# Two quarters of a weight transform moved into the groups that use them, in a gated scan and Hadamard feed-forward kernel

## The chip, the cores and the metric

The kernel runs on one core of one Trainium2 chip, with its engines TensorE (PE; PEld is its weight load), VectorE (DVE), ScalarE (ACT), GpSimd (POOL) and SyncE (SP, which here only issues DMAs). The metric is device microseconds of one execution. Everything is float32.

## What is computed

Four sequences of 512 tokens with 512 channels pass a gated linear scan and then a feed-forward block with 2048 hidden channels, each with a normalized residual. Cut to what matters:

```python
x = x + layernorm(attn(layernorm(x)))
x = x + layernorm(ffn(layernorm(x)))

def attn(h):                       # h: (4, 512, 512)
    i, f, g = h @ Wi.T, h @ Wf.T, h @ Wg.T
    gate = sigmoid(f)
    v = silu(i) * (1 - gate)
    o = scan over tokens: o[t] = gate[t] * o[t-1] + v[t]
    return (rmsnorm(o) * gnorm_w * g * sigmoid(g)) @ Wo.T

def ffn(x):                        # W1, W3: (2048, 512); W2: (512, 2048)
    hidden = silu(x @ W1.T) * (x @ W3.T)
    hidden = walsh_hadamard(hidden)         # along 2048 channels, / sqrt(2048)
    return hidden @ W2.T
```

## The kernel before

Every large product is done by the seven-product scheme for 2x2 block matrices (Strassen in Winograd's form): `ORDER` names the products P1, P2, P6, P5, P7, P3, P4 with their left and right operands. Of the left operand's seven blocks A11, A12, A21, A22 are data and S1, S2, S4 sums (`combine_left`; S3 takes A21's place); of the right operand's, B11, B21, B22, B12 are data and T1, T2, T4 sums (`combine_right`; T3 takes B12's place). A product adds into one of three PSUM banks X, Y, Z; after each product a copy on ScalarE (the first into a target) or an addition on VectorE takes the bank to SBUF: line 524 or 522 in projections and output products, 960 or 963 in the paired groups.

The Hadamard transform is not applied to the hidden channels but to W2, on which it works as well. Its high part is done by matmuls in the first 100 us and written to the DRAM tensor `w2_h`. The low part is done per quarter p = 0..3 of 512 hidden channels: `load_low(p)` loads four pieces of 256 KB (line 1109) into two tiles, `low_pair(p)` adds and subtracts the two tiles (lines 1120 and 1121, four VectorE instructions), and `low_tile(m)` makes the seven blocks of a tile's right operand in place (lines 1127 to 1134: five VectorE instructions and one on ScalarE), and writes them to DRAM (`kept`, line 179, issued by GpSimd, 896 KB). `again` (line 186) reads such a kept tile back.

The order of the work, by sequence (batch) b:

- `attn_unit(b, u)` for u = 0, 1, 2 projects with Wi, Wf, Wg; `attn_out(b)` multiplies by Wo. Work given to `fill` is put between the products of a unit; work in `beside` stands at a named product of it, behind an instruction that `behind(...)` names.
- Batches 0 and 1 do the first half of the hidden channels alone: `solo_unit(b, m)`, m = 0..3, with `ffn_out(b, 0)` and `ffn_out(b, 1)` for the first two quarters of W2. Batch 3's attention (units at about 226 to 290 us) lies between `solo_unit(0, 3)` and `solo_unit(1, 0)`.
- The rest is done for two sequences at once by `ffn_pair`, with one more level of the seven-product scheme over the pair. `GROUPS = 2, 3, 0, 1, 2, 3`: groups at = 0 and 1 are quarters 2 and 3 for the pair (0, 1), groups 2 to 5 all four quarters for the pair (2, 3). The first group starts at about 356 us, the second at 425, the third at 493.

A group has seven steps (`OUTER`: P1, P2, P6, P7, P5, P4, P3), each of seven products ("leaves", 1 to 49 in a group). A step's left operand is a "leaf weight" (tag "w" of the pool `stream`): four pieces of 128 KB are loaded per step from the kept W1 and W3 by `load_leaf_w`, three steps ahead, and summed on GpSimd. Its right operand is a token block: `xq[B11]`, `xq[B21]`, and so on, each of seven inner blocks. `blocks[0]` holds the pair B11 and B12, `blocks[1]` B21 and B22, `blocks[2]` T2 and T1; T4 has a tile of its own. Raw differences (`raw`, `combine_pair_early`, `combine_pair_late`) make T2, T1, T3, T4 out of the four data blocks, and `inner` makes the inner sums of a token block, in this kernel for the two blocks of a pair in one instruction. The dictionary `events` gives what is put behind a leaf. Between the leaves stand the output products of the group before (`down`, `ffn_out` in pieces). After steps 5 and 6, `hidden` multiplies the gates into the tiles `ht` (line 930), whose inner sums GpSimd makes.

The third quarter's low transform is loaded before `attn_unit(3, 0)` and done beside `attn_unit(3, 1)`; the last quarter's beside `solo_unit(1, 0)`. Both are kept in DRAM, and `load_down_pair(2)` and `load_down_pair(3)` read them back at leaf 14 of the groups 0 and 1.

W1 and W3 of the hidden channels' second half are prepared in eight calls of `prepare()` from `solo_unit(0, 3)` to `solo_unit(1, 3)`: load two of 256 KB into a tile of `stream` (lines 198), sum on VectorE (`combine_weights`, lines 158 to 163), write to DRAM (line 179).

Buffers: `stream` has five tiles (unit weights, prepared weights, leaf weights), `stream2` four (W2's quarters and Wo). The tag "wide" of the pool `work` has three: outputs of the two sequences (`f_0`, `f_1`) hold two of them through the pair's two groups; the third goes from an attention output `y` to the normalized rows of batch 3 (`xn_f_3`, written to DRAM at line 317) and, in the second group, to the first fold of the next pair (`load_half_fold(0)`). A "fold" is a reload of normalized rows from DRAM in the order in which VectorE transposes them (line 460 loads, 485 transposes).

TensorE's and SP's instructions run in the order in which the program gives them. Those of VectorE, ScalarE and GpSimd are put in order by a planner, with its own estimates of when each is ready, priorities (`tc.high_priority`) and "not before" edges (`tc.issue_after`); on the chip each engine then runs its list in order. A DMA issued on SP waits there until its tile is free, and everything behind it on SP waits too.

Of the kernel before, what the change touches and what calls it, by code (L numbers as in the profile page):

```python
# [11 lines left out]
F32 = mybir.dt.float32  # L12
# [32 lines left out]
def kernel(  # L45
# [119 lines left out]
    def combine_right(t, eng, steps=(0, 1)):  # L165

        if 0 in steps:
            eng.tensor_sub(t[:, T1], t[:, B12], t[:, B11])
            read["T2"] = eng.tensor_sub(t[:, T2], t[:, B22], t[:, T1])
        if 1 in steps:  # L170
            eng.tensor_sub(t[:, T3], t[:, B22], t[:, B12])
        if 0 in steps:
            eng.tensor_sub(t[:, T4], t[:, B21], t[:, T2])

    def kept(key, t):

# [4 lines left out]
    def stream_tile(key, b, pool=stream):  # L181
        return pool.tile([P, 7, H], F32, tag="w", name="_".join(map(str, (*key, b))))
# [3 lines left out]
        nc.sync.dma_start(out=t, in_=saved[key])  # L186
        return t

    def weight(src, name, m, b):

        key = name, m
        if key in saved:
            return again(key, b).rearrange("p s (c f) -> p s c f", c=2)
        t = stream_tile(key, b)
        half = src.shape[1] // 2
        for h in range(2):
            cols = slice(h * half + m * P, h * half + (m + 1) * P)
            nc.sync.dma_start(
                out=t[:, 2 * h : 2 * h + 2].rearrange("p k (c f) -> p (k c) f", c=2),
                in_=src[:, cols].rearrange("(p c) f -> p c f", p=P),  # L200
            )
        uncombined.append((key, t))
        return t.rearrange("p s (c f) -> p s c f", c=2)
# [600 lines left out]
    def raw(r):  # L804
        return xq[r][:, 0:4]

    def inner(pair, steps=(0, 1), eng=None):
        combine_right(pair.rearrange("p r s f -> p s r f"), eng or nc.vector, steps)

    def combine_pair_early():  # L810

# [286 lines left out]
    def load_low(p):  # L1098


        ms = range(p * NS, (p + 1) * NS)
        if p == 1:
            pair = work.tile([P, NS, 7, H], F32, tag="og", name="w2_23")
            tiles = [pair[:, k] for k in range(NS)]
        else:
            tiles = [stream_tile(("w2", m), 0, stream2) for m in ms]
        for n, k in ((1, 4), (0, 0)):
            for m, t in zip(ms, tiles):
                nc.sync.dma_start(
                    out=t[:, k : k + 2].rearrange("p k f -> p (k f)"),  # L1110
                    in_=w2_h[:, n * NU + m, :],
                )
        for m, t in zip(ms, tiles):
            down_w[0, m] = low_w[m] = t

    def low_pair(p):

# [188 lines left out]
    def prepare():  # L1306
        name, m = LATER.pop(0)
        weight(SOURCE[name], name, m, 0)
# [48 lines left out]
    attn_unit(3, 1)  # L1357
    combine_soon()
# [6 lines left out]

    places = (1, "P2"), (4, "P7"), (6, "P3")
    fill.extend([None] * 4 + attn_out(3))
    load_low(3)
    spread_low(3, "P2", 0)
    prepare()  # L1370
    solo_unit(1, 0, True)
    for b in PAIR:
# [13 lines left out]
        + [lambda: [make() for make in early]],  # L1386
        places,
    )
    prepare()
    solo_unit(1, 2)  # L1390
    fill.extend([None] + ffn_out(1, 0))
    pair_beside([partial(inner, blocks[0]), partial(inner, blocks[1], (0,))], places)
    prepare()
    for k in range(AHEAD):
        load_leaf_w(k)
    solo_unit(1, 3)
# [1 line left out]
        folds.pop(("f", b))  # L1398


    late = combine_pair_late()
# [14 lines left out]
    def exchange():  # L1416
# [3 lines left out]
    ffn_pair(  # L1420
        1,
        down,
        {
            7: [partial(load_half_fold, 0)],
            9: [partial(load_half_fold, 1)],
            14: [partial(load_down_pair, 3)],
            29: [transpose_half(0, 0, half_fold(0, 0))],
            31: [transpose_half(1, 0, half_fold(1, 0))],
            37: [exchange, transpose_half(0, 1, half_fold(0, 1))],
            39: [transpose_half(1, 1, half_fold(1, 1))],  # L1430
            43: [partial(early_step, 0)],
            45: [partial(early_step, 1)],
            47: [partial(early_step, 2)],
            49: [partial(early_step, 3)],
        },
        28,
    )
# [8 lines left out]
    PAIR[:] = 2, 3  # L1446
    for at in range(2, len(GROUPS)):
        g = GROUPS[at]
        ffn_pair(at, deque(down), {**late, 24: [partial(load_down_pair, g)]})
        late = {}  # L1450
        down = [part for b in PAIR for part in ffn_out(b, g, True)]
    for b in PAIR:
# [35 lines left out]
```

## Time and profile before

| what | value |
|---|---|
| time, median of 3 runs | 799.63 us (798.67 to 799.67) |
| profiled execution, its own time | 800.42 us |
| its span, first to last instruction | 798.6 us |
| mean granted TensorE clock | 0.991 |
| PE busy | 768.2 us (96%), 3552 matmuls |
| PEld busy | 662.4 us (83%) |
| DVE busy | 615.9 us (77%), 1157 instructions |
| ACT busy | 238.2 us (30%) |
| POOL busy | 350.5 us (44%) |
| DMA | 149.12 MB, 187 GB/s over the span |
| kept tile to DRAM (line 179, 896 KB) | 24 times, median 7.7 us from issue to landing |
| prepared or unit weight from the inputs (256 KB) | 32 times, 5.9 us |
| leaf weight piece (128 KB) | 168 times, 2.4 us |
| low transform piece (256 KB) | 16 times, 8.1 us |

Busy shares of the span in five stretches, worked out from the windows' sums (the last column is the mean granted clock):

| stretch, us | what runs | PE | DVE | POOL | clock |
|---|---|---|---|---|---|
| 200 to 264 | end of batch 0's solo units, batch 3's first attention units | 58.0 of 64.0 | 48.8 | 12.6 | 1.00 |
| 264 to 355.8 | rest of batch 3's attention, batch 1's solo units | 89.0 of 91.8 | 76.9 | 13.9 | 1.00 |
| 355.8 to 425.4 | first group of the first pair | 65.3 of 69.6 | 55.4 | 44.1 | 0.95 |
| 425.4 to 493.1 | second group | 67.3 of 67.7 | 54.2 | 47.9 | 1.00 |
| 493.1 to 560 | third group's first part | 64.8 of 66.9 | 55.9 | 51.3 | 1.00 |

A row of a view names the source line, the engine, the operation, and what is written from what (out<-in). A wait is written as who waited and for whom. An instruction's row in a timeline may merge several of one kind; its length then goes from the first to the last.

### The profile page before, as it was taken

What the parts mean: (1) busy time and instruction counts of PE and PEld (TensorE: products, weight loads), DVE (VectorE), ACT (ScalarE), POOL (GpSimd) and SP (SyncE); (2) the same over time, 40 slices, a digit from 0 to 9 for tenths busy, and PEclk for the clock granted to TensorE, in tenths of its full rate; (3) what the DMA queues carried; (4) which work ended last, traced back from release to release, by engine and by line L of the source; (5) the groups of instructions that cost most, each with busy time, mean ns of one, the idle gap of its engine ahead of it and who ended that gap; (6) DMA issues with size and microseconds to landing.
All of it is one profiled execution on the core that took longest, in us unless ns stands there. A gap on an engine that the chain in (4) does not pass through costs nothing.

```text
span 798.6 us, 10396 instructions
## 1 busy us (share of the span) xinstructions
PE 768.2 (96%) x3552; PEld 662.4 (83%) x3552; DVE 615.9 (77%) x1157; ACT 238.2 (30%) x332; POOL 350.5 (44%) x429
## 2 busy tenths in 40 slices
PE   9999999999998999897999999899999999999994
PEld 7888688887887788786888888788888788888884
DVE  6789889799686797899767599977755655765686
ACT  5373745535534332324111111021230201121112
POOL 2111203013202100048469558957966865682452
PEclk9999999999999999999999999999999999999998
DMA  9997556885998989868229320243455141124012
GB/s 302 398 340 294 168 195 224 264 277 198 372 323 302 347 319 325 327 225 303 74 66 253 87 57 27 74 136 94 106 171 132 53 143 55 54 70 154 1 53 105
DMA packets 93908, 149.12 MB, mean 187 GB/s; under 512 B 15136, under 2 KB 72096, under 8 KB 93600
## 3 DMA queue, kind: packets, MB, share of 16 engines
q1 hardware_dynamic: 82992, 97.87, 39.4%
q0 software_dynamic: 10144, 49.29, 17.0%
q10 hardware_dynamic: 720, 1.31, 0.4%
q8 instruction: 28, 0.46, 0.2%
q14 instruction: 24, 0.20, 0.1%
HBM read 100.21 MB, written 50.33 MB: 188 GB/s over the span
## 4 chain that ended last, share of the span: by engine, by line
PE 75%; DVE 11%; DMA 7%; POOL 2%; issue 2%; SPq 1%; ACT 1%; POOLq 0%; DVEq 0%
PE X_u L950 16%; PE X_po L715 10%; PE X_a L547 8%; PE Z_u L950 8%; PE Z_po L715 5%; PE X_f L547 5%; PE Z_a L547 4%; PE Y_u L950 4%; PE X_y L655 3%; PE Y_po L715 2%; PE Y_a L547 2%; PE Z_f L547 2%; DMA wl<-s_w 2%; DMA fold_a<-xnd_a 2%; PE Z_y L655 2%
## 5 line engine op out<-in xcount | busy, mean ns | idle before, releaser
L715 PE MATMUL X_po<-w,ht 128*128 128x256 f32 x512 | 140.8, 383 | 0.4 <-DVE f L522 0.3
L963 DVE TENSOR_TENSOR q<-X_u,q 128x512 f32<-128x512 f32 x132 | 90.7, 687 | 52.2 <-PE X_u L950 50.0
L950 PE MATMUL X_u<-xq,wl 128*128 128x256 f32 x480 | 123.6, 381 | 4.8 <-ACT q L960 2.8
L715 PEld LDWEIGHTS X_po<-w,ht 128*128 128x128 f32 x512 | 98.3, 192 | 14.8 <-DVE f L522 1.2
L950 PEld LDWEIGHTS X_u<-xq,wl 128*128 128x128 f32 x480 | 91.2, 191 | 18.7 <-DVE q L963 2.8
L921 ACT ACTIVATE q<-q 128x1024 f32<-128x1024 f32 x24 | 25.4, 1058 | 157.8 <-DVE q L963 89.0
L878 POOL TENSOR_TENSOR q<-q,q 128x512 f32<-128x512 f32 x48 | 60.6, 1277 | 26.2 <-DVE q L963 24.4
L715 PE MATMUL Z_po<-w,ht 128*128 128x256 f32 x256 | 69.1, 379 | 1.0 <-ACT f L524 1.0
L963 DVE TENSOR_TENSOR q<-Z_u,q 128x512 f32<-128x512 f32 x72 | 49.6, 689 | 25.5 <-PE Z_u L950 24.6
L179 POOL DMA_DIRECT2D s_w<-w x24 | 13.1, 547 | 118.6 <-DVE w L163 89.8
L547 PE MATMUL X_f<-xt_f,w 128*128 128x256 f32 x256 | 60.6, 381 | 4.1 <-DMA w<-s_w 2.7
L960 ACT COPY q<-X_u 128x512 f32<-128x512 f32 x36 | 21.0, 585 | 143.6 <-PE X_u L950 139.4
L950 PE MATMUL Z_u<-xq,wl 128*128 128x256 f32 x240 | 61.6, 379 | 0.0
L547 PEld LDWEIGHTS X_f<-xt_f,w 128*128 128x128 f32 x256 | 48.2, 190 | 11.8 <-DMA w<-s_w 3.1
L715 PEld LDWEIGHTS Z_po<-w,ht 128*128 128x128 f32 x256 | 48.5, 190 | 8.1 <-ACT f L524 1.4
L950 PE MATMUL X_u<-og,wl 128*128 128x256 f32 x192 | 50.1, 384 | 2.3 <-DVE q L963 2.2
L950 PEld LDWEIGHTS Z_u<-xq,wl 128*128 128x128 f32 x240 | 45.6, 190 | 6.2
L158 POOL TENSOR_TENSOR wl<-wl 128x256 f32<-128x256 f32 x42 | 33.6, 800 | 38.7 <-DMA wl<-s_w 32.1
L522 DVE TENSOR_TENSOR f<-X_po,f 128x512 f32<-128x512 f32 x51 | 34.9, 683 | 12.5 <-PE X_po L715 11.7
L950 PEld LDWEIGHTS X_u<-og,wl 128*128 128x128 f32 x192 | 36.7, 193 | 8.8 <-POOL wl L163 2.6
L963 DVE TENSOR_TENSOR q<-Y_u,q 128x512 f32<-128x512 f32 x42 | 28.8, 687 | 19.2 <-PE Y_u L950 17.8
L930 DVE TENSOR_TENSOR ht<-q 128x512 f32<-128x512 f32 x48 | 38.3, 820 | 5.3 <-PE X_po L715 4.1
(221 smaller groups left out, 1573.1 us busy)
## 6 DMA issues: line engine op xcount, KB each, us to landing
s_w<-w POOLq DMA_DIRECT2D x24, 896.0 KB, 7.7
w<-s_w SPq DMA_DIRECT2D x24, 896.0 KB, 7.3
wl<-s_w SPq DMA_DIRECT2D x168, 128.0 KB, 2.4
w<-in_W_dram SPq DMA_DIRECT2D x32, 256.0 KB, 5.9
wi<-s_wi SPq DMA_DIRECT2D x6, 896.0 KB, 8.8
wf<-s_wf SPq DMA_DIRECT2D x6, 896.0 KB, 8.1
wg<-s_wg SPq DMA_DIRECT2D x6, 896.0 KB, 7.1
w_h<-w2p POOLq DMA_DIRECT2D x8, 512.0 KB, 5.8
```

Source lines behind the costliest of these rows:

```text
L158: eng.tensor_add(t[:, S1], t[:, A21], t[:, A22])
L179: nc.gpsimd.dma_start(out=saved[key], in_=t)
L522: read[what] = nc.vector.tensor_add(to, ps[which], to)
L547: nc.tensor.matmul(ps[:, n, :], w[:, a, c, :], xt[:, bb, c, :], start=first and n == 0 and c == 0, stop=c == 1, skip_group_check=True,)
L655: nc.tensor.matmul(ps[:, t, :], og[:, a, c, ts(t, P)], w[c][:, bb, :], start=first and t == 0 and c == 0, stop=c == 1, skip_group_check=True,)
L715: nc.tensor.matmul(ps[:, t, :], hts[b, m][:, a, ts(t, P)], w[m][:, W2[bb], :], start=first and k == 0, stop=m == ms[-1], skip_group_check= ...
L878: queued.append(make(*args).ins)
L921: nc.scalar.activation(d[:, 0], d[:, 0], AF.Silu)
L930: nc.vector.tensor_mul(t[:, h : h + 3 : 2], d[:, 0, n].rearrange("p (t f) -> p t f", t=2), d[:, 1, n].rearrange("p (t f) -> p t f", t=2),)
L950: nc.tensor.matmul(ps[which][:, k, :], w[:, k, a, :], x[:, bb, :], start=first and k == 0, stop=True, skip_group_check=True,)
L960: read["copy"] = nc.scalar.copy(y, ps[which])
L963: last = nc.vector.tensor_add(y, ps[which], z)
```

## The change

1. *Low transform.* `load_low`, `low_pair` and `low_tile` of quarter 2 leave batch 3's attention units and become events of the first group (load at leaf 6, pair at 17, tiles at 19 and 23). Those of quarter 3 leave `solo_unit(1, 0)` and become events of the second group (leaves 1, 10, 12, 14). The tiles are used where they are made, for both sequences (`down_w[1, m]` too), and are still written to DRAM for the second pair. `load_down_pair` at leaf 14 of the two groups is gone.
2. *Inner sums.* `inner` takes one token block instead of a pair. B11's are made beside `solo_unit(1, 3)`; those of B21, T2, B12, T1, T4, B22 become events at leaves 2 to 35 of a pair's first group. For the second pair, B11's first three are made on GpSimd (behind leaf 36 of the second group) and the fourth on VectorE at leaf 45; the two calls behind the second group are gone.
3. *Prepared weights.* The last two (W1 and W3 of m = 7) are no longer prepared in `stream` beside `solo_unit(1, 2)` and `solo_unit(1, 3)`. `prepare_wide` loads them into tiles of the tag "wide": the first before the first group's first leaf, the second at leaf 14; their sums stand at leaves 13 and 25.
4. *Batch 3's attention input.* Its four normalizing copies stand at earlier products ((0, 3), (0, 4), (0, 6), (1, 0) in place of (0, 4), (0, 5), (1, 0), (1, 3), where the pair is unit and product), and `load_fold(3, "a", "x")` goes ahead of `load_attn_w(3, 0)`.

```diff
-    def weight(src, name, m, b):
+    def weight(src, name, m, b, t=None):
...
-        t = stream_tile(key, b)
+        if t is None:
+            t = stream_tile(key, b)
...
-    def inner(pair, steps=(0, 1), eng=None):
-        combine_right(pair.rearrange("p r s f -> p s r f"), eng or nc.vector, steps)
+    def inner(r, steps=(0, 1), eng=None):
+        return combine_right(xq[r], eng or nc.vector, steps)
...
             1: [partial(sub, raw(T2), raw(B21), raw(T4))],
-            2: [partial(sub, raw(T1), raw(B22), raw(T2))],
-            4: [partial(inner, blocks[1], (1,))],
-            6: [partial(inner, blocks[2], (0,))],
-            8: [partial(inner, blocks[2], (1,))],
-            11: [partial(combine_right, xq[T4], nc.vector)],
+            2: [partial(inner, B21, (0,))],
+            5: [partial(sub, raw(T1), raw(B22), raw(T2))],
+            7: [partial(inner, B21, (1,))],
+            9: [partial(inner, T2)],
+            15: [partial(inner, B12)],
+            21: [partial(inner, T1)],
+            28: [partial(inner, T4)],
+            35: [partial(inner, B22)],
...
-            down_w[0, m] = low_w[m] = t
+            down_w[0, m] = down_w[1, m] = low_w[m] = t
...
-    late = dict(beside_copies(3, ((0, 4), (0, 5), (1, 0), (1, 3))))
+    late = dict(beside_copies(3, ((0, 3), (0, 4), (0, 6), (1, 0))))
...
+    load_fold(3, "a", "x")
     load_attn_w(3, 0)
-    load_fold(3, "a", "x")
     load_low(1)
...
     load_attn_w(3, 1)
-    load_low(2)
...
-    spread_low(2, "P2", 0)
...
-    load_low(3)
-    spread_low(3, "P2", 0)
...
-    prepare()
     solo_unit(1, 2)
     fill.extend([None] + ffn_out(1, 0))
-    pair_beside([partial(inner, blocks[0]), partial(inner, blocks[1], (0,))], places)
-    prepare()
+    pair_beside([partial(inner, B11)], places)
...
+    def low_beside(p, leaves):
+        makes = [partial(load_low, p), partial(low_pair, p)]
+        makes += [partial(low_tile, NS * p + t) for t in range(NS)]
+        return {leaf: [make] for leaf, make in zip(leaves, makes)}
+
+    def prepare_wide():
+        name, m = LATER.pop(0)
+        t = work.tile([P, 8, H], F32, tag="wide", name=f"{name}_{m}", bufs=3)
+        weight(SOURCE[name], name, m, 0, t[:, 0:7])
+
     load_down_w(1, 1)
+    prepare_wide()
+    late = merged(
+        combine_pair_late(),
+        {13: [combine_weights], 14: [prepare_wide], 25: [combine_weights]},
+        low_beside(2, (6, 17, 19, 23)),
+    )
...
-    ffn_pair(0, deque(down), {**late, 14: [partial(load_down_pair, 2)]})
+    ffn_pair(0, deque(down), late)
...
-            14: [partial(load_down_pair, 3)],
...
+            36: [partial(in_order, inner, B11, (0,), nc.gpsimd)],
...
-            45: [partial(early_step, 1)],
+            45: [partial(inner, B11, (1,)), partial(early_step, 1)],
...
-        },
+        }, low_beside(3, (1, 10, 12, 14))),
         28,
     )
-    with tc.high_priority(offset=SOON):
-        inner(blocks[0])
-        inner(blocks[1], (0,))
```

`merged` joins several such dictionaries, leaf by leaf; `combine_right` now returns the instruction that it issues last.

More of the change, by code (lines that the diff above doesn't have):

```diff
@@ L172, in combine_right @@
         if 0 in steps:
-            eng.tensor_sub(t[:, T4], t[:, B21], t[:, T2])
+            return eng.tensor_sub(t[:, T4], t[:, B21], t[:, T2])
     def kept(key, t):
@@ L830, in combine_pair_late, with merged @@
             1: [partial(sub, raw(T2), raw(B21), raw(T4))],
-            2: [partial(sub, raw(T1), raw(B22), raw(T2))],
-            4: [partial(inner, blocks[1], (1,))],
-            6: [partial(inner, blocks[2], (0,))],
-            8: [partial(inner, blocks[2], (1,))],
-            11: [partial(combine_right, xq[T4], nc.vector)],
-        }
+            2: [partial(inner, B21, (0,))],
[6 more added lines that the diff above has]
+            35: [partial(inner, B22)],
+        }
+    def merged(*plans):
+        events = {}
+        for plan in plans:
+            for leaf, makes in plan.items():
+                events.setdefault(leaf, []).extend(makes)
+        return events
     def pair_beside(makes, places):
@@ L1398 @@
         folds.pop(("f", b))
-    late = combine_pair_late()
-    load_down_w(1, 1)
+    def low_beside(p, leaves):
[6 more added lines that the diff above has]
+        weight(SOURCE[name], name, m, 0, t[:, 0:7])
+    load_down_w(1, 1)
+    prepare_wide()
[4 more added lines that the diff above has]
+    )
     down = [make for make in fill if make] + ffn_out(1, 1, True)
     fill.clear()
-    ffn_pair(0, deque(down), {**late, 14: [partial(load_down_pair, 2)]})
+    ffn_pair(0, deque(down), late)
     down = deque(part for b in PAIR for part in ffn_out(b, 2, True))
@@ L1422 @@
         down,
-        {
+        merged({
             7: [partial(load_half_fold, 0)],
             9: [partial(load_half_fold, 1)],
-            14: [partial(load_down_pair, 3)],
             29: [transpose_half(0, 0, half_fold(0, 0))],
             31: [transpose_half(1, 0, half_fold(1, 0))],
+            36: [partial(in_order, inner, B11, (0,), nc.gpsimd)],
             37: [exchange, transpose_half(0, 1, half_fold(0, 1))],
@@ L1448 @@
         g = GROUPS[at]
-        ffn_pair(at, deque(down), {**late, 24: [partial(load_down_pair, g)]})
+        ffn_pair(at, deque(down), merged(late, {24: [partial(load_down_pair, g)]}))
         late = {}
```

## The prediction

> **What bounds the kernel now.** I read the page first: TensorE is busy 768.2 of 798.6 us, and its 3552 matmuls come every 0.216 us where nothing is late (8 in 1.73 us in the chain that ended last). 3552 x 0.216 = 767, so all there is to win is some 31 us in which TensorE stands or runs at a lower clock. Next I read what TensorE waited for. The columns are us in total, times, longest.
>
> ```profile
> PE X_u L950 <- DVE q L963: 4.2, 2, 2.2
> PE X_a L547 <- ACT d_a L524: 3.1, 1, 3.1
> PE X_u L950 <- ACT q L960: 2.8, 2, 2.1
> PE X_f L547 <- DMA w<-s_w: 2.7, 1, 2.7
> PE X_a L547 <- DVE d_a L522: 1.5, 1, 1.5
> PE X_a L547 <- issue: 1.4, 1, 1.4
> PE X_f L547 <- DVE d_f L522: 1.4, 1, 1.4
> ```
>
> The timeline gives their places: 224.3 (the 1.4 of "issue": batch 3's first product, whose fold landed at 225.5), 253.6 (3.1), 262.2 (1.5), 336.2 (2.7), 359.0 (2.1), 375.1 (2.2) and 501.1 (2.0). Outside what the diff touches are 186.5 (1.4) and 632.6 (0.7). Inside: 1.4 + 3.1 + 1.5 + 2.7 + 2.1 + 4.2 = **15.0 us**. Then I asked for windows at the seven steps of the first pair's first group (columns: us; busy of PE, PEld, DVE, ACT, POOL; granted clock; DMA share; GB/s).
>
> ```profile
> 355.80:372.76 16.96, 14.87 (x62) 12.49 (x60) 16.36 (x29) 6.45 (x9) 11.71 (x13) 0.90 0.84 274
> 372.76:385.12 12.36, 10.12 (x39) 8.33 (x38) 11.24 (x18) 2.49 (x4) 8.62 (x10) 0.86 0.59 229
> 385.12:393.32 8.20, 8.20 (x39) 7.22 (x38) 6.85 (x12) 1.06 (x1) 2.83 (x4) 1.00 0.23 67
> 393.32:401.09 7.77, 7.77 (x37) 6.84 (x36) 3.23 (x5) 1.75 (x3) 2.83 (x4) 1.00 0.22 68
> 401.09:409.30 8.21, 8.21 (x40) 7.22 (x39) 4.98 (x8) 0.58 (x1) 6.21 (x5) 1.00 0.22 65
> 409.30:417.50 8.20, 8.20 (x40) 7.22 (x39) 5.30 (x9) 1.06 (x1) 6.58 (x8) 1.00 0.24 66
> 417.50:425.44 7.94, 7.94 (x37) 6.76 (x36) 7.39 (x12) 1.06 (x1) 5.35 (x7) 1.00 1.02 197
> ```
>
> Steps 0 and 1 are full of VectorE work (27.6 of 29.3 us) and lose clock: the granted clock is 0.60 in 362-366 and in 379-383, so another 2 x 4 x 0.4 = **3.2 us**. Steps 2 to 6 leave VectorE 12.6 us idle (1.35 + 4.54 + 3.23 + 2.90 + 0.55). What the change can touch is 15.0 + 3.2 = 18.2 us.
>
> Here a rule stands against a row. The Trainium skill, "TensorE: Matmul & The Clock Gate", section on the HAM clock gate, lets the clock fall only after an idle window of about 3.4 us. Here it fell after waits of 2.1 and 2.2 us and stayed at 1.00 around those of 3.1 and 2.7. By the rule the clock would have nothing to give back; I go by the rows.
>
> **The change part by part.** Four rows of timelines (start, length, engine) show the mechanisms.
>
> ```profile
> 248.34 0.43 DVE L158 TENSOR_TENSOR w<-w 128x256 f32<-128x256 f32 x1 [6.39 <-DMA w<-in_W_dram]
> ...
> 324.09 10.63 SPq L186 DMA_DIRECT2D w<-s_w  x2
> ...
> 359.47 2.35 DVE L562 TENSOR_TENSOR ht<-d_f 128x1024 f32<-128x1024 f32 x2
> ...
> 360.77 0.59 ACT L960 COPY q<-X_u 128x512 f32<-128x512 f32 x1 [4.15 <-DVE ht L562]
> ```
>
> (1) *Batch 3's fold goes ahead of wi and wf on SP, its normalizing copies three products earlier.* The last copy ran at 204.1; it moves to about where the third now runs, 195.4. Copy 1.3, then write to landing 4.8 (205.7 to 210.5), give about 202; the tile it goes to is free at 202.7 (landing of batch 1's last kept x). Four issues end near 206 instead of 217.9, and the fold lands near 215 instead of 225.5. The 1.4 us go. wi, issued at 190.7, now waits behind the fold until 206; landing in 8.8 it is there at 215, needed at 226: nothing.
>
> (2) *The third quarter's low transform leaves batch 3's units.* On VectorE that is four pair instructions of 0.68, and per tile one of 0.68 and four of 0.42: 2.7 + 2 x 2.4 = 7.4 us, at 255-268, where VectorE is busy 9.97 of 10 us. The wait at 262 (1.5) should go; I take 1.4. The wait at 253.6 is another: VectorE stood 6.39 us on a prepared weight, with the gates' instruction behind it. That weight's load stood on SP until 241.6 for the write of the one before, itself loaded at 221.6 behind the late fold. With (1) it comes some 10 us sooner, so the hold is covered. Ends 0 and 3.1, as the order on VectorE may change; I take 2.3.
>
> (3) *Two weights fewer through the five stream tiles.* The 10.63 us above are unit (1,3)'s second weight: its tile is freed by a prepared weight's write that landed at 334.35. Without the last two prepared weights the tiles of unit (1,1) serve, free at 322.8; the first of the two landed 9.5 after its issue, which would be 334 for this one, before 336.2. Ends 0 and 2.7, I take 2.4.
>
> (4) *VectorE ahead of and in steps 0 and 1.* Eight combining instructions (0.41 to 0.95) and seven two-block instructions (0.68 to 3.02) in 334-358 become four single ones of 0.42. The 2.35 us of line 562 then start when SiLU ends, at 356.2, not 359.5; ScalarE's copy behind them frees TensorE: the 2.1 go. In steps 0 and 1 the inner sums cost 7.2 us by their rows, now 8 x 0.42 = 3.4, and 0.8 of a weight's sums goes: 27.6 becomes 23.0. There are 98 matmuls, 21.2 us, so 1.8 stay over. Of 2.1 + 2.2 + 3.2 = 7.5 I take 5.0 (ends 2.1 and 7.5).
>
> (5) *After the second group.* The seven two-block instructions at 488-502 (0.67 to 1.21) go; GpSimd takes three single ones, 0.9 each, where it is busy 0.00 of 7.84 us (472-480); without that cover they would hold the leaf weights by 2.7. Of the 2.0 at 501 I take 1.8.
>
> Gains: 1.4 + 1.4 + 2.3 + 2.4 + 5.0 + 1.8 = **14.3 us**.
>
> (6) *What VectorE gets instead.* Steps 2 to 6: low transform 7.4, two weights' sums 8 x 0.42 = 3.4, sixteen inner instructions 6.7, together 17.5 for 12.6 idle; 4.9 run over into the second group's steps 0 to 4, idle 2.4 + 2.8 + 2.3 + 4.6 + 0.5 = 12.6, which get the last quarter's 7.4: 12.3 of 12.6. That just fits. But GpSimd is busy there (44.1 of 69.6 us), and the rows show what this does: the instruction of 3.02 us at 345.1 (0.68 elsewhere) spans three GpSimd instructions. The inner sums of steps 0 and 1 took 7.2 us where the same shapes cost 5.1 elsewhere, 1.4 times. 24.9 x 0.4 = 10.0, less 0.3 of room: 0 to 9.7 us. I take 2.5, since PSUM additions are planned ahead of all this and the last quarter isn't needed before the third group.
> The Trainium skill, "SBUF — State Buffer", section "Who interferes with whom", speaks against the change: an instruction of VectorE with two SBUF inputs and a reading one of GpSimd block one another entirely. At GpSimd's share of 0.63 it would make the added instructions half as long again or more, some 12 us for 0.3 of room.
>
> (7) *A chain through one tile.* Both late weights use the one free "wide" tile, after batch 3's normalized rows. From the group's start: second write issued at 15 (375.3 - 355.8 less 4.3 of stalls), landed 21; load 5.9: 27; sums 1.7; write 8.3: 37; load 6.5: 44; sums and write 10: 54; issue and landing of the next group's first leaf 4.2: 58, needed at 61. SP works in program order, so leaf 3 (needed at 29) issues at 22 and lands at 27; leaf 5 (needed at 44) issues at 38, lands at 42. Each just fits. Should VectorE's order have a late load at its head, the PSUM additions of line 963 stand behind it, and TensorE behind them. Between 0 and 6; I take 0.5.
>
> (8) Four reloads of 896 KB go; the DMA share there is 0.22 to 0.25, so nothing.
>
> **Sum:** -14.3 + 2.5 + 0.5 = -11.3. The profiled execution took 800.42 us (span 798.6 and 1.8 around it), 0.8 above the median of 799.63; from the median the forecast is **788 us**.
>
> **The rivals.** *All waits go and nothing comes:* 18.2 us, 781. For it: the sums of (6) fit without slowing. Against: steps 0 and 1 stay over-full. *VectorE's crowding only moves:* (4) gives 2.1, (6) costs 9.7, the rest stays: 14.3 - 2.9 - 9.7 = 1.7, near 798; with the 2.3 of (2) failing, 800. For it: both groups end without idle time. Against: 385-417 ran without a wait. *Slower: VectorE's order holds for late DMAs in the first group.* Three steps there are fed by DMA (two weights, the low transform). A hold like the 6.39 us of 248 costs less one leaf of cover, 0.9: 5.5, and with clock loss 1.6: 7.1. Three make 21.3 against 14.3: 806.6; from two on (14.2) the change gains nothing. For it: (7)'s chain has two writes of 7.7, the kind whose lateness made that hold. Against: between 200 and 520 us only two loads held VectorE above 1 us, 1.36 and 6.39.
>
> **How the numbers follow.** Forecast 0.55 (own range 783 to 794), all gone 0.20, moved 0.12, slower 0.13. 0.2% is 1.6 us, about what a measurement here can tell from no change. Moved gives 0.04 faster, 0.06 same, 0.02 slower: faster 0.79, same 0.06, slower 0.15. The range reaches from 779 (781, and 2 of the waits outside) to 801, which leaves out most of the slower case.
>
> **What would show it.** Right: no TensorE wait above 1 us between 220 and 345; clock 1.00 through the first pair; VectorE nearly full in both groups. Wrong: VectorE idle over 3 us for a DMA in the first group; a leaf's first product waiting for its load at steps 3 or 5 or at the next group's start; a lowered clock in steps 2 to 6.

## The result and the profile after

The changed kernel takes 812.39 us (median of 4, 811.62 to 813.29) against 799.65 us (798.67 to 802.23) for the kernel before on the same chip: ratio **1.0155, interval 1.0129 to 1.0181**. It is slower by 12.7 us; the forecast was 788 us. The profiled execution took 813.29 us, its span is 811.5 us. Ratios here and below are the record's own, over fast executions (one of e4 and one of b2, of 3808.61 and 4638.19 us, are left out as slow), and are not quotients of the medians shown.

First the page after: busy time and instructions of the engines, and the two rows of slices (each slice is 20.3 us) that differ from before.

```profile
PE 769.2 (95%) x3552; PEld 661.6 (82%) x3552; DVE 618.4 (76%) x1178; ACT 237.8 (29%) x332; POOL 353.2 (44%) x432
...
PE   9999999999989999999749999999999899999994
PEclk9999999999999999999959999999999999999998
```

TensorE does the same 3552 matmuls in the same busy time. One stretch, near 400 to 426 us, holds the loss: it is busy 0.7 and 0.4 there, and its clock fell. The view of what TensorE waited for (us in total, times, longest), after:

```profile
PE X_u L961 <- DVE q L974: 17.4, 4, 15.0
PE X_f L548 <- DVE d_f L523: 2.6, 2, 1.4
PE X_u L961 <- ACT q L971: 2.5, 2, 1.7
PE Z_po L716 <- ACT f L525: 2.0, 1, 2.0
PE X_a L548 <- DVE d_a L523: 2.0, 1, 2.0
PE X_a L548 <- ACT d_a L525: 1.8, 1, 1.8
```

Of the waits that the change was to remove, those at 224, 262, 336, 359, 375 and 501 are gone. But 253 kept 1.8 of 3.1, new ones of 2.0, 1.2 and 1.7 stand at 241.1, 347.9 and 384.7, and at 402.7 TensorE stands for **15.05 us** in one piece. (Places are where TensorE stops; the prediction's are 0.4 us early, its 253.6 is 254.0 in the trace.) (Lines 961, 974, 971, 548 are 950, 963, 960, 547 of before.) The windows of the first group's seven steps, after (columns as in the prediction):

```profile
352.66:365.61 12.95, 12.95 (x62) 11.40 (x61) 12.00 (x22) 3.99 (x7) 5.62 (x5) 1.00 0.10 31
365.61:373.81 8.20, 8.20 (x40) 7.21 (x38) 6.39 (x13) 0.59 (x1) 1.84 (x3) 1.00 0.57 189
373.81:382.43 8.62, 8.46 (x40) 7.06 (x39) 8.62 (x17) 2.60 (x3) 2.04 (x3) 1.00 0.27 109
382.43:392.15 9.72, 8.00 (x37) 6.76 (x36) 7.78 (x18) 5.38 (x7) 2.02 (x3) 1.00 0.42 146
392.15:400.35 8.20, 8.20 (x39) 7.22 (x38) 8.20 (x17) 1.00 (x2) 2.52 (x3) 1.00 0.95 306
400.35:426.91 26.56, 11.51 (x40) 9.30 (x39) 10.82 (x19) 1.01 (x1) 18.91 (x22) 0.68 0.33 115
426.91:434.88 7.97, 7.97 (x37) 6.76 (x36) 7.42 (x12) 1.11 (x2) 7.18 (x10) 1.00 0.35 96
```

Steps are counted from 0, as in the prediction. Leaf weights are too: weight 7, called leaf 7 below, is that of the next group's step 0, while a number in an edit, as in "at leaf 14", is a place between products. Read by step: steps 0 and 1 fell from 29.3 to 21.15 us, all that 98 matmuls need; step 5, from 400.35, grew from 8.2 to 26.56. The group starts 3.1 us sooner than before (352.66 for 355.79), takes 82.2 us instead of 69.65, and the second takes 70.6 instead of 67.7: -3.1 + 12.6 + 2.9 = 12.4, and some 0.5 in the rest, is the 12.9 by which the span grew.

The chain behind the 15 us, from timelines of the changed kernel by engine (start, length, engine, line; in brackets the idle time before and what ended it), oldest first:

```profile
376.77 0.59 POOL L179 DMA_DIRECT2D s_w<-w  x1 [1.51 <-DVE w L163]
...
380.89 4.96 ACT L309 ACTIVATE xn_f<-x,nb_f,rs_f 128x512 f32<-128x512 f32 x4 [5.46 <-DVE q L974]
...
386.15 0.73 POOL L318 DMA_DIRECT2D xnd_f<-xn_f  x1 [1.69 <-ACT xn_f L309]
...
389.49 1.22 SPq L199 DMA_DIRECT2D w<-in_W_dram  x2
390.81 24.05 SPq L900 DMA_DIRECT2D wl<-s_w  x20
...
398.95 0.95 DVE L163 TENSOR_TENSOR w<-w 128x256 f32<-128x256 f32 x1
...
404.58 1.10 POOL L179 DMA_DIRECT2D s_w<-w  x2
412.85 0.72 POOL L158 TENSOR_TENSOR wl<-wl 128x256 f32<-128x256 f32 x1 [7.17 <-issue]
...
415.69 5.05 POOL L889 TENSOR_TENSOR q<-q,q 128x512 f32<-128x512 f32 x4
...
416.98 0.69 DVE L974 TENSOR_TENSOR q<-X_u,q 128x512 f32<-128x512 f32 x1 [10.12 <-POOL q L889]
...
417.72 2.08 PE L961 MATMUL X_u<-xq,wl 128*128 128x256 f32 x4 [15.05 <-DVE q L974]
```

W1's late weight (the first `prepare_wide`) was loaded at 346.18 into the one free wide tile. Its sums stand at leaf 13, so it was written only at 376.77; that write landed at 380.74. Only then was the tile free for batch 3's normalized rows: four copies on ScalarE, two writes, the last landed at 389.35. Only then could SyncE issue the load of W3's late weight (389.49), and the leaf loads of leaves 5 and 6 stood behind it on SyncE. Its sums ended at 399.90, its write went out near 405 and landed at 410.73. Leaf 7, the next group's first, needs it in its fourth piece (issued 410.75, landed 412.72). GpSimd sums leaf 7 (412.85), **and behind that, in its fixed order, come the eight additions of the current group's step 4, P5 (line 889)**, which VectorE and then TensorE wait for in step 5. SyncE's own waits in the changed kernel show the two holds that this chain made (us in total, times, longest): 12.5 us before leaf 7's fourth piece (398.2 to 410.7; the longest of this kind before was 8.1), and 18.7 before the second weight's load (to 389.4; before has no such row for the weights' line):

```profile
SPq L900 <- DMA s_w<-w: 21.4, 2, 12.5
SPq L199 <- DMA xnd_f<-xn_f: 21.2, 2, 18.7
```

After the wait the clock costs more: windows of the changed kernel, 402.5 to 426.

```profile
402.50:417.70 15.20, 0.17 (x1) 0.00 (x0) 5.05 (x9) 0.00 (x0) 7.86 (x11) 0.64 0.56 198
...
420.00:422.00 2.00, 2.00 (x6) 1.63 (x5) 0.60 (x1) 0.00 (x0) 1.92 (x2) 0.50 0.00 0
...
424.00:426.00 2.00, 2.00 (x11) 1.77 (x10) 1.31 (x2) 0.10 (x1) 1.92 (x3) 1.00 0.00 0
```

From 417.7 to 423.9 the granted clock is 0.50 and matmuls come every 0.43 us: 6.2 x 0.5 = 3.1 us more. Wait, clock and the 1.7 at 384.7 make 19.9 of the 20.8 us that steps 2 to 6 gained in length.

### The profile page after: what moved, and what is told of

It reads as the page before. It is cut to its first block, busy times and chain, and to the rows that moved or that the text cites. A ratio compares the mean times of both kernels' runs of the same rounds, so it can differ in the third digit from the quotient of the medians.

```text
span 811.5 us, 10426 instructions
## 1 busy us (share of the span) xinstructions
PE 769.2 (95%) x3552; PEld 661.6 (82%) x3552; DVE 618.4 (76%) x1178; ACT 237.8 (29%) x332; POOL 353.2 (44%) x432
## 5 line engine op out<-in xcount | busy, mean ns | idle before, releaser
L889 POOL TENSOR_TENSOR q<-q,q 128x512 f32<-128x512 f32 x48 | 61.0, 1286 | 20.8 <-DVE q L974 19.1
L974 DVE TENSOR_TENSOR q<-Z_u,q 128x512 f32<-128x512 f32 x72 | 49.4, 686 | 22.0 <-PE Z_u L961 21.7
L158 POOL TENSOR_TENSOR wl<-wl 128x256 f32<-128x256 f32 x42 | 34.5, 822 | 51.8 <-DMA wl<-s_w 20.3
L548 PEld LDWEIGHTS X_f<-xt_f,w 128*128 128x128 f32 x256 | 48.2, 190 | 10.3 <-DVE d_f L523 3.3
L523 DVE TENSOR_TENSOR f<-X_po,f 128x512 f32<-128x512 f32 x51 | 34.8, 683 | 12.4 <-PE X_po L716 10.6
```

The lines of the kernel that those rows point to most:

```text
L158: eng.tensor_add(t[:, S1], t[:, A21], t[:, A22])
L523: read[what] = nc.vector.tensor_add(to, ps[which], to)
L548: nc.tensor.matmul(ps[:, n, :], w[:, a, c, :], xt[:, bb, c, :], start=first and n == 0 and c == 0, stop=c == 1, skip_group_check=True,)
L889: queued.append(make(*args).ins)
L974: last = nc.vector.tensor_add(y, ps[which], z)
```

## The experiments

The theory that the trace suggests is the **chain** above: tile, two writes, SyncE, and GpSimd's order. The rival is **crowding**: VectorE is full in steps 2 and 4 (8.62 of 8.62, 8.20 of 8.20) since it got the low transform and the sums, so everything is late. Edits are to the changed kernel, or, in the runs named "alone", to the kernel before. Ratios are to runs of the kernel before on the same chip (medians 799.65 us for the changed kernel, 800.56 for e1 to e4, 800.48 for e5 and p1 to p3, 800.96 for p4, b1 and b2). The last column is the length of the first group in us, from the profiled execution; it is 69.65 in the kernel before.

| run | us, median | ratio | interval | first group |
|---|---|---|---|---|
| changed kernel | 812.39 | 1.0155 | 1.0129 to 1.0181 | 82.2 |
| W1's sums early (e1) | 807.27 | 1.0079 | 1.0052 to 1.0106 | 76.5 |
| leaf 7 after the additions (e2) | 806.06 | 1.0063 | 1.0037 to 1.0090 | 75.7 |
| no low sums (e3) | 806.71 | 1.0060 | 1.0039 to 1.0082 | 77.0 |
| weights in stream (e4: parts 1, 2, 4) | 801.53 | 0.9994 | 0.9968 to 1.0020 | 68.6 |
| both sums early (e5) | 803.16 | 1.0046 | 1.0026 to 1.0066 | 73.2 |
| part 1 alone (p1) | 800.70 | 1.0000 | 0.9983 to 1.0017 | 68.3 |
| part 2 alone (p2) | 796.71 | **0.9943** | 0.9909 to 0.9977 | 64.4 |
| part 3 alone (p3) | 813.80 | **1.0173** | 1.0129 to 1.0217 | 81.5 |
| part 4 alone (p4) | 803.86 | 1.0042 | 1.0021 to 1.0063 | 69.9 |
| parts 2 and 4 (b1) | 798.05 | 0.9983 | 0.9963 to 1.0003 | 64.4 |
| 2, 4, and 3 with both sums early (b2) | 798.33 | 0.9982 | 0.9963 to 1.0002 | 67.7 |

**e1, W1's sums at leaf 1.**

```diff
-        {13: [combine_weights], 14: [prepare_wide], 25: [combine_weights]},
+        {1: [combine_weights], 14: [prepare_wide], 25: [combine_weights]},
```

> The first wide weight's sums stand at leaf 1 of the first group and not at leaf 13; all else is the changed kernel. Chain theory (the 15.0 us wait in step 5 is GpSimd standing before the sums of leaf weight 7, which waits for the second wide weight, which waits for batch 3's normalized rows, which wait for the first wide weight's tile): the first weight is written 15 us earlier, the chain ends before step 4's additions, the wait falls under 2 us and the lowered clock behind it goes: 812.4 - 14 to 18 = 794 to 798 us. Crowding theory (VectorE has more to do in the first group than fits): the same work stands at another place, 810 to 815 us.

The second load went out at 374.56 instead of 389.49, 15 us sooner, and the wait fell only from 15.05 to 8.99. The sums of the second weight did not follow: planned at leaf 25, they ended after 399, as before. A link was loosened, the next one held.

**e2, leaf 7's sums behind step 4's additions on GpSimd.**

```diff
-        in_order(combine_left, t.rearrange("p w s f -> p s w f"), nc.gpsimd)
+        def sums():
+            in_order(combine_left, t.rearrange("p w s f -> p s w f"), nc.gpsimd)
+
         leaf_w[n] = t
+        if n == 7:
+            return sums
+        sums()
...
-            load_leaf_w(7 * at + step + AHEAD)
+            held = load_leaf_w(7 * at + step + AHEAD)
...
+            if held:
+                held()
```

> The sums of leaf weight 7 (the second group's first) are queued on GpSimd behind step 4's additions and not ahead of them; loads, VectorE and SP are as in the changed kernel. Chain theory: the weight is as late as before (landing near 413 us), but nothing of this group stands behind it; the 15.0 us wait falls under 2 us, the next group starts near 416 with up to 3 us of wait for the sums: 794 to 800 us. Crowding theory: no change, 811 to 814 us.

GpSimd's timeline in this run:

```profile
402.95 0.72 POOL L163 TENSOR_TENSOR wl<-wl 128x256 f32<-128x256 f32 x1
403.63 1.26 POOL L889 TENSOR_TENSOR q<-q,q 128x512 f32<-128x512 f32 x1
404.84 1.09 POOL L179 DMA_DIRECT2D s_w<-w  x2
405.95 9.73 POOL L889 TENSOR_TENSOR q<-q,q 128x512 f32<-128x512 f32 x7
```

The additions start at 403.63, before the weight is even written; so it was leaf 7's sums that held them at 415.69. The 15 us became 3.70 + 3.62: the sums of leaves 5 and 6 still end at 403.6, since their loads stood on SyncE behind the late weight's load (in e1, where that load went out 15 us sooner, they end at 388.9), and eight additions of 1.3 us then run back to back beside leaves that take 1.2 each.

**e3, without the third quarter's low transform on VectorE.** The quarter's pair and tile sums are left out (ScalarE copies blocks in their place), so this kernel computes less.

```diff
+        if p == 2:
+            return
...
+        if m in (4, 5):
+            nc.scalar.copy(t[:, 2:4], t[:, 0:2])
+            nc.scalar.copy(t[:, 6], t[:, 4])
+            kept(("w2", m), t)
+            return
```

> Leaves out the third quarter's low transform on VectorE (four pair instructions and ten tile instructions, 7.4 us, in the first group); ScalarE copies blocks in their place, and loads and writes stay. Chain theory: the second weight's sums, spread over 394.2 to 399.9 in the changed kernel, come together and some 4 us earlier; the wait shrinks from 15 to 9 to 12 us: 805 to 810 us. Crowding theory: 7.4 us of VectorE work less and the wait goes with it: 797 to 803 us.

The load of the second weight goes out at 390.27, no sooner than after (389.49); only what follows it on VectorE is quicker (written at 401.28 instead of 404.58 to 405.7). The wait is 6.78. Without the largest new load on VectorE 0.60 of the 1.55% is left: crowding lengthens the chain (the first addition starts at 415.69 with it and at 410.20 without), and some three fifths of the loss go with it. That it does not make the chain is shown by p3 below, not by this run.

**The relation.** In the five runs where TensorE stands more than 3 us at this place, it goes on 2.03 to 2.04 us after GpSimd's first addition starts, whatever was edited:

| run | leaf 7's sums | first addition | TensorE goes on | its wait |
|---|---|---|---|---|
| after | 412.85 | 415.69 | 417.72 | 15.05 |
| p3 | 415.57 | 418.41 | 420.45 | 8.54 |
| e1 | 407.40 | 410.23 | 412.27 | 8.99 |
| e3 | 407.36 | 410.20 | 412.24 | 6.78 |
| e2 | behind | 403.63 | 405.67 | 3.70 |

The rows behind the last two columns, here of e1:

```profile
402.25 1.03 PE L961 MATMUL Y_u<-xq,wl 128*128 128x256 f32 x4
412.27 2.08 PE L961 MATMUL X_u<-xq,wl 128*128 128x256 f32 x4 [8.99 <-DVE q L974]
```

**e4, part 3 undone.**

```diff
+    prepare()
     solo_unit(1, 2)
...
+    prepare()
...
-    prepare_wide()
...
-        {13: [combine_weights], 14: [prepare_wide], 25: [combine_weights]},
```

> Undoes one part alone: the last two weights are prepared in the stream tiles again, beside the two solo units, and nothing of them is left in the first group. Chain theory: no chain through the wide tile, so the 15.0 us wait goes; in return waits for stream tiles come back (2.7 us at 336 in the kernel before, part of the 2 + 2 us in steps 0 and 1): 794 to 800 us. Crowding theory: only 3.4 us of the 17.5 us added to VectorE in the first group go: 806 to 810 us.

The 15 us are gone, no wait of TensorE in the first group is above 1.7, and the wait for a stored weight near 334 is back (2.5; the 1.8 of the first row stands in the third group):

```profile
PE X_u L961 <- DVE q L974: 5.9, 5, 1.8
PE X_f L548 <- DMA w<-s_w: 2.5, 1, 2.5
```

The time is that of the kernel before.

**p3, part 3 alone in the kernel before.**

> The kernel before with one part of the change alone: the last weight pair through the wide tile, sums at leaves 13 and 25; the low transforms stay where they were and are read back. Chain theory: the chain needs nothing of the other parts, so the wait on GpSimd in steps 4 and 5 shows here too, 8 to 15 us long, and the waits for stream tiles before the group go (2.7 and part of 4): 803 to 812 us. Crowding theory: only 3.4 us of VectorE work are added to the group: 796 to 801 us.

It gives the whole loss (the intervals overlap). GpSimd's and TensorE's timelines of this run show the same order with no low transform beside it:

```profile
405.66 0.72 POOL L158 TENSOR_TENSOR wl<-wl 128x256 f32<-128x256 f32 x1 [9.12 <-DMA wl<-s_w]
...
415.57 0.72 POOL L158 TENSOR_TENSOR wl<-wl 128x256 f32<-128x256 f32 x1 [3.45 <-DMA wl<-s_w]
...
418.41 10.19 POOL L886 TENSOR_TENSOR q<-q,q 128x512 f32<-128x512 f32 x8
...
420.45 2.07 PE L958 MATMUL X_u<-xq,wl 128*128 128x256 f32 x4 [8.54 <-DVE q L971]
```

The wait in step 5 is shorter than after, 8.54, because steps 0 and 1 are still over-full there (27.0 us) and TensorE comes later; the chain's end, 63.1 us after the group's start, is the same (415.69 - 352.66 = 63.0 after). Not all of the loss is this wait: one of 3.9 us for an addition of VectorE stands in step 0 too, at 365.9. Still, the loss comes with part 3 (p3), goes without it (e4), and its wait shrinks to 3.7 when one entry of GpSimd's queue is moved (e2): the chain is confirmed, and crowding by the moved transform is refuted as the main cause.

**p1 and p2, the first two parts alone.**

> The kernel before with the low transforms of the last two quarters moved into the first two groups and used in place, nothing else of the change. Chain theory: no wide weight, so no wait above 3 us in the first group beyond those of the kernel before; the wait at 262 goes: 796 to 801 us. Crowding theory: 7.4 us of VectorE work in each group, on top of steps 0 and 1 that are over-full: 804 to 812 us.

> The kernel before with the inner sums block by block alone (B11's first three on GpSimd for the second pair). Both theories: VectorE is relieved in steps 0 and 1, part of the 2.1 + 2.2 us and of the 3.2 us of lost clock goes, and the 2.0 at 501; the second group may lose 1 to 2 us where GpSimd has B11's sums to make: 794 to 800 us.

p1 is neutral. Its first group is 1.3 us shorter, it starts 1.5 us sooner, and the second group gives it back (70.3 for 67.7). p2 is faster than both kernels. Its windows of steps 0 and 1:

```profile
354.67:367.62 12.95, 12.95 (x62) 11.40 (x61) 12.44 (x25) 7.47 (x10) 9.49 (x11) 1.00 0.99 323
367.62:376.35 8.73, 8.43 (x39) 7.13 (x38) 6.76 (x12) 1.82 (x2) 5.72 (x8) 1.00 0.97 342
```

21.7 us for the 29.3 of before, at full clock. This is the gain that the change was made for, and it needs only one of its four parts.

**e5, both sums early (leaves 1 and 18).**

```diff
-        {13: [combine_weights], 14: [prepare_wide], 25: [combine_weights]},
+        {1: [combine_weights], 14: [prepare_wide], 18: [combine_weights]},
```

> As the run with the first weight's sums at leaf 1, and the second wide weight's sums at leaf 18 in place of 25 (its load landed at 379 there, and its sums lay at 393.5 to 400). Chain theory: the write starts near 385 and not at 400.4, leaf weight 7 is loaded and summed before step 4's additions are due at 394; the 9.0 us wait that was left falls under 2 us and the lowered clock goes: 794 to 799 us. Crowding theory: the same VectorE work, earlier in the fullest stretch: 805 to 812 us.

The first addition starts at 403.13, 12.6 us sooner, and the waits shrink to 1.4, 1.5, 1.5 and 2.9. But it missed the kernel before. Here crowding does show. From 384.03 to 401.73 VectorE is busy 17.70 of 17.70 us, and its four sums of the second weight take from 385.5 to 391.2, between instructions of the low transform. In the next step, GpSimd's additions and VectorE's sums slow one another: the additions take up to 1.51 us, for 1.25 to 1.27 after, and VectorE's timeline reads:

```profile
402.18 0.41 DVE L168 TENSOR_TENSOR xq<-xq 128x256 f32<-128x256 f32 x1
...
408.71 1.48 DVE L168 TENSOR_TENSOR og<-og 128x256 f32<-128x256 f32 x1
410.11 0.68 DVE L974 TENSOR_TENSOR q<-Z_u,q 128x512 f32<-128x512 f32 x1
410.71 2.52 DVE L169 TENSOR_TENSOR og<-og 128x256 f32<-128x256 f32 x1
```

An instruction of 0.41 us took 1.48 and 2.52; the PSUM addition between them, which reads one of its inputs from PSUM, kept its 0.68.

**b2, the same without part 1.** The kernel before with parts 2 and 4, and part 3 with its sums at leaves 1 and 18; both low transforms stay where they were.

> The changed kernel with the sums of the two late weights at leaves 1 and 18, and without part 1 (both low transforms stay where they were before; their tiles are read back at leaf 14). With part 1 in, this was 1.0046, and TensorE still waited 1.4, 1.5, 1.5 and 2.9 us in the first group's steps 3 to 5. Theory A: those waits were VectorE's crowding by the third quarter's low transform, which held the second late weight's sums from 379 to 391 and shared the path with GpSimd's additions; without it the weight is written by 387, no leaf load waits more than 4 us on SyncE for it, the first group takes 65 to 67 us, ratio 0.991 to 0.994, 793 to 796. Theory B: the chain through the one wide tile is too long whatever VectorE does; SyncE still stands about 10 us before that weight's piece, TensorE waits 4 us or more in step 5, the first group takes 70 us or more, ratio 1.000 to 1.005.

Neither theory fully. TensorE waits in steps 3 to 5 fell to 0.5 and 0.3 us, as A said, but SyncE still stood 8 us (390.8 to 398.8) for the weight's write, as B said: with the first addition at 403.83 and TensorE there only at 408, a chain of this length just fits. The group took 67.7 us, above A's 65 to 67, and the ratio, 0.9982, stands above A's range; a 2.4 us wait at 363.1 for GpSimd's leaf sums and the loss of part 4 account for part of it. Between e5 and b2, part 1 costs 0.64% once part 3 is in, though alone it costs nothing.

**p4 and b1, part 4 alone and with part 2.**

```diff
-    late = dict(beside_copies(3, ((0, 4), (0, 5), (1, 0), (1, 3))))
+    late = dict(beside_copies(3, ((0, 3), (0, 4), (0, 6), (1, 0))))
...
+    load_fold(3, "a", "x")
     load_attn_w(3, 0)
-    load_fold(3, "a", "x")
```

> The kernel before with part 4 alone (batch 3's fold ahead of wi and wf, its copies three products earlier). If the parts simply add, the wait of 1.4 to 1.6 us at 224 goes and nothing else changes: 0.998 of the kernel before, near 798.9. Rival: the prepared weight behind the fold comes no sooner, and the order on VectorE around 240 to 255 gives the same time back: ratio 1.000, with a wait of 1 to 3 us of TensorE on d_a at 240 to 263 that is longer than before by what 224 lost.

> The kernel before with parts 2 and 4, without parts 1 and 3. Part 2 alone gave 0.9943. If part 4 adds its 1.5 us, 0.9925, near 794.6, and the first group takes 64 to 66 us. Rival: part 4's gain is given back before the first group; then 0.994 to 0.995, near 796.

The rivals were right that the gain is given back, and short of what came: p4 is at 1.0042, not 1.000, and b1 at 0.9983, not 0.994 to 0.995. What TensorE waited for in p4:

```profile
PE X_a L547 <- ACT d_a L524: 2.9, 1, 2.9
...
PE X_a L547 <- DVE d_a L522: 1.9, 1, 1.9
```

The wait at 224 went and one of 1.9 came at 241.0; those at 255 and 260 (before 253 and 262) stayed. The reason is in the windows of 212 to 242, here of p4:

```profile
212.00:226.00 14.00, 13.90 (x64) 11.65 (x62) 7.40 (x19) 5.12 (x8) 1.64 (x3) 1.00 1.01 338
226.00:242.00 16.00, 15.00 (x69) 12.84 (x68) 15.97 (x35) 5.53 (x9) 1.10 (x2) 1.00 0.99 372
```

TensorE gains 1.2 us before 226 (busy 13.90 for 12.69) and gives back 0.9 by 242 (15.00 for 15.86), since VectorE was full there in both kernels (15.97 and 15.95 of 16). About 1.6 us are lost at the group's start (357.42 for 355.79). The rest of p4's 0.42% stands in the third and fourth groups (1.4 and 2.8 us longer), which part 4 doesn't touch. The granted clock is 0.50 there for 3.41 us twice, from 505.45 and from 624.92, behind waits of 2.0 and 2.15 us; in the kernel before it stayed at 1.00 behind the wait of 2.0 at 501.5, and the other wait was 1.0. The last section says what decides this; it is no property of part 4. b1's ratio is what p2 and p4 add up to (0.9985).

The four parts alone add up as well: 0.00 - 0.57 + 1.73 + 0.42 = 1.58%, and the change made 1.55%. (Each has an interval of some 0.2 to 0.4% to either side.) Best of all is p2, 0.9943: the single tokens' inner sums, and nothing else of the change. No run joins e1 and e2, or gives the two late weights a tile of their own, so whether part 3 can be had without loss beside the others stays open.

## Why the prediction was wrong

**The step that failed is (7).** It followed the right chain and asked the right question, when leaf 7's last piece lands and when it is needed. It said "58, needed at 61" after the group's start, and priced the chain at 0.5 (0 to 6). The landing was nearly right: 412.72 - 352.66 = **60.1**. That was luck, errors that cancel: the order in the tile was W1's weight, batch 3's rows, W3's weight, and not the rows first. The need was wrong. I took it from TensorE, the next group's first product. But leaf 7 goes through GpSimd, whose order `in_order` fixes, and its sums are put ahead of step 4's additions. TensorE was ready for those at 402.67, 15.05 before it went on, so to cost nothing the piece had to land by 412.72 - 15.05 = 397.67, **45.0** after the group's start, and not by 61. It landed at 60.1. Leaf 7 is not alone in this: the sums of leaves 5 and 6, whose loads the same chain held on SyncE, end at 404.6, too late as well, and with leaf 7 out of the way (e2) 3.70 and 3.62 us stayed. The step called it a fit because it looked at what is queued behind a late load on VectorE ("the PSUM additions of line 963 stand behind it, and TensorE behind them") and not on GpSimd. With the wait at 15.1 and 3.1 of clock, the prediction's sum becomes -14.3 + 2.5 + 18.2 = +6.4, on the slow side; the rest up to +12.7 is mainly what (1), (2) and (5) did not bring.

Step by step, for the rest:

- **(1) fold ahead, 1.4: wrong.** The error was "the tile it goes to is free at 202.7". The fold's first load was released at 211.04 before and at 211.20 in p4 by the same thing, a normalizing copy on ScalarE of other rows (L308, 209.7 to 211.0). It landed at 221.6 instead of 225.5, not at 215, and VectorE, full until 242, took the gain back.
- **(2) third quarter's transform out of batch 3, 2.3: half right.** The wait at 262 went. "Some 10 us sooner" for the prepared weight was wrong: its load stood at 241.21 for 241.60 before, behind the write of the weight before it, which VectorE, full since 226, summed no sooner. The hold on VectorE stayed and 253 kept 1.8. What part 1 earns here is not separated: in p1 both waits are gone and the group starts 1.5 sooner, but in p2 and p3, which leave these units alone, 253 is gone too and 0.5 and 1.0 are left of 262. The row of the hold, after:

```profile
250.92 0.42 DVE L158 TENSOR_TENSOR w<-w 128x256 f32<-128x256 f32 x1 [5.99 <-DMA w<-in_W_dram]
```

  Steps (1) to (3) had 6.1 us together; the group's start came 3.1 sooner.
- **(3) two weights fewer in `stream`, 2.4: right in the changed kernel.** The 2.7 at 336 went, and came back (2.5) when e4 undid the part. Alone the part does not earn it: in p3 three waits of 1.0 to 1.2 for stored weights stand at 302 to 324. A gain bought with a wait six times its size.
- **(4) VectorE in steps 0 and 1, 5.0 with an upper end of 7.5: right in kind, too small.** The steps fell by 8.2 (29.3 to 21.15), and by 7.6 in p2. I had left 1.8 us over by a sum of VectorE's work; the planner moved that work on into steps 2 to 5, where p2 gives back 2.4 (42.8 us in steps 2 to 6 for 40.3).
- **(5) after the second group, 1.8: not got.** The wait at 501 went, but one of 1.6 stands at 559.1 (in p2 1.7 at 540.8), one group later. Why it comes back there was not tried.
- **(6) crowding, 2.5 (0 to 9.7): the range was right.** Part 1 alone costs nothing in sum (1.0000), but only because it gains ahead of the groups what it costs in them. In p1 the second group takes 70.3 us for 67.7; beside parts 2 and 4 (e4 against b1) the first group starts 4.3 us sooner, and the two groups take 4.2 and 2.4 more (68.6 for 64.4, 70.6 for 68.2). All seven runs with part 1 have a second group of 70.3 to 71.2, all six without it one of 67.7 to 68.2. Beside part 3 it also lengthens the chain, and costs 0.64%, some 5 us. The Trainium skill, "SBUF — State Buffer", section "Who interferes with whom", says that a VectorE instruction with two SBUF inputs and a GpSimd instruction that reads SBUF block one another, and one with a single SBUF input does not. The rows of e5 agree for VectorE: 0.41 became 1.48 and 2.52, and the PSUM additions stayed at 0.68. GpSimd's additions lost less, at most 1.51 for 1.27.
- **(8) reloads, nothing:** no run separates it.

The rival "slower: VectorE's order holds for late DMAs" had the sign (806.6), but not the mechanism: VectorE did not stand in front of a DMA in the first group; its 10.12 us were a wait for GpSimd. Of the signs named, "a lowered clock in steps 2 to 6" came true, and "a leaf's first product waiting for its load at steps 3 or 5" named the right step, though what TensorE waited for there was an addition and not a load.

## What to carry to other kernels

When a step makes a load later, its need is not where its data is used but the first point where something else is queued behind it, on each engine that works in a fixed order: here a tile for the next group stood in GpSimd's queue ahead of additions for the current one, which moved the due time from 61 to 45 us. Where several transfers share one tile, write down the chain tile by tile with the order that the kernel really takes, and let the one with the earliest need go first; loosening one link (e1) gains only as far as the next. And take a change of several parts apart: here one of four parts carries all the gain.

## What was not expected of the hardware

- The clock. A wait of one size lowered it or not: in p4 TensorE waited 2.2 us at 361.0 and kept 1.00, and 2.3 us at 376.7 and fell to 0.50; in the kernel before, waits of 2.1 and 2.2 lowered it, and 3.1 and 2.7 did not. The traces show what decides. Four windows of the kernel before, 1 us each:

```profile
361.00:362.00 1.00, 0.50 (x2) 0.48 (x3) 1.00 (x2) 0.84 (x2) 1.00 (x2) 0.88 0.89 258
...
365.00:366.00 1.00, 1.00 (x6) 0.86 (x5) 1.00 (x2) 1.00 (x3) 1.00 (x2) 0.91 0.96 395
...
378.00:379.00 1.00, 1.00 (x6) 0.81 (x6) 0.91 (x3) 0.00 (x0) 0.29 (x1) 0.91 1.06 372
...
382.00:383.00 1.00, 1.00 (x6) 0.90 (x5) 1.00 (x2) 0.00 (x0) 1.00 (x2) 0.88 0.00 0
```

  A mean of 0.88 in a window that ends at 0.50 means a fall at 361.76; read so, the clock is low from 361.76 to 365.18 and from 378.82 to 382.24. Both stretches are 3.41 us long, and they begin 5 x 3.41 us apart. It is so in all 13 traces between 150 and 780 us: a low stretch lasts 1, 2, 3 or 5 times 3.41 us (6.83 in p1, 10.24 in e1, 17.07 after), and the falls of one run lie whole multiples apart (p4: 379.16, 505.45 and 624.92, that is 37 and 35). So time is cut into cells of 3.41 us that run on whatever TensorE does, and what counts is how long TensorE stands within one cell. The clock fell at the end of every cell with 2.0 us or more of waiting, stayed up after every one with 1.8 or less, and did either between 1.89 and 1.94. It came back at the end of a cell with at most 0.33 us of waiting, and stayed low after cells with 0.61 or more. The 2.2 us in p4 that cost nothing lie across two cells (1.05 and 1.14), and so do the 3.1 at 254.0 in the kernel before (1.94 and 1.18). The Trainium skill, "TensorE: Matmul & The Clock Gate", section "What's actually happening", says that the window of about 3.4 us runs freely. These traces agree with the length and with that; but here the window need not be idle throughout for the clock to fall: 2.0 of 3.41 us were enough.
- Where the DMA share was 1.05 to 1.09 a prepared weight's halves of 256 KB took 8.4 to 10.3 us from issue to landing (p4 and before, 220 to 232 us), and 2.9 to 3.6 where it was 0.48 and 0.66 (after, 346.2 to 350.3 and 389.5 to 393.3).
